# How the recurrent state is turned and split into float16 halves: casts and two transposing transfers, in place of block transposes and a way through DRAM

## Chip, cores and metric

The kernel runs on one core of a Trainium2 chip, alone. The metric is the time of one execution in microseconds (us) of device time; the number given for a kernel is the median of several runs.

## What is computed

Two graph layers work on `x`, 32 batches of 512 nodes with 128 features, over one adjacency matrix `adj` of 512 x 512. Each layer normalises its input, applies a ReLU, and adds its result to its input. Layer 0 is graph attention. Layer 1 is a gated recurrence of five steps, and the change lies in it:

```python
def step(h, _):
    m_in = jnp.einsum('nm,bmd->bnd', in_matrix, h)
    m_out = jnp.einsum('nm,bmd->bnd', out_matrix, h)
    av = jnp.concatenate([m_in, m_out], axis=-1)
    u3 = h @ u3_w.T + u3_b
    z = jax.nn.sigmoid(av @ w3_w.T + w3_b + u3)
    r = jax.nn.sigmoid(av @ w4_w.T + w4_b + u3)
    hv = jnp.tanh(av @ w5_w.T + w5_b + (r * h @ u5_w.T + u5_b))
    h = (1.0 - z) * h + z * hv
    return (h, None)
```

Both matrices are `adj` here, so one product `m` serves for both, with the two halves of each weight added up beforehand.

## The kernel before

**Tiles.** A batch is one tile of 128 partitions x 512 columns. The state `h` of a batch is needed in two layouts. With features on the partitions and nodes along the columns it is `hT` (float32, 128x512); all gates and the update work on that. With nodes on the partitions it is the weight operand of the product with the adjacency, and there it stands as two float16 tiles `hi` and `lo` (128 x 4 x 128): `hi` is `h` rounded to float16, `lo` is what is left, rounded too. Their two products are added in one PSUM bank, so the matmuls run in float16 and the result keeps nearly float32's precision. Ten slots of `hT`, `hi`, `lo` and `x1` (the layer's input) let up to ten batches be under way.

**One step of one batch** (`recurrence`, L1013 to L1222): four matmuls with `hi` and four with `lo` (L1032) make `m`; ACT copies it to `mT` (L1043); two matmuls make the gate `r` (L1051, L1052), ACT takes the tanh (L1057), DVE makes `rh` (L1064); a third matmul makes `z` (L1072), ACT its tanh (L1084); two matmuls make the candidate `v` (L1095, L1096), ACT takes its tanh (L1102), and three DVE instructions update `hT` (L1109, L1115, L1118). Then `hT` has to be turned for the next step.

**Three ways of turning.** For the first batches and for the last two steps of the last four batches, TensorE transposes `hT` into PSUM (L1156). The very last batch has an `ending` of its own (L1224), in two half tiles. All other steps, 118 before a next step and 28 after the last one, go this way: DVE transposes 32x32 blocks (L1170, tile `blocks`), SP stores them to a DRAM tile `way` (L1176), and four loads on SP bring them back with the blocks in place (L1181, tile `rows`, 32 partitions each). Where a next step follows, `halves` (L1002) makes `hi` from `rows` on ACT (L1009) and `lo` on DVE (L1007). After the last step, ACT (L1205) and DVE (L1208) make the result from `rows` and SP stores it (L1221). Layer 0 has a similar way of its own, through the POOL queue (L734, L747), and is not touched.

**The order of the work** is not left to a scheduler. Every piece of work is a `Task` with an engine, a cost from the table `COST`, its needs, its buffers, a key (when it is due) and `lands`, the delay after which others see its result. `plan` (L84) plays the tasks forward: at each turn it takes, on the engine that can begin first, the task with the lowest key among those that can begin nearly as early, and the list of begin times becomes the fixed program order of each engine. A transfer has `lands=LANDING`, 5000 ns. Sixty-eight dummy transposes (`idle`, L435) have the highest key, so that they are put wherever TensorE has nothing else in the plan. A `Buffer` is taken from a pool whose size stands in `BUFFERS`; the plan waits for one to come free. So a change of one piece of work can give another order everywhere behind it.

```python
order = plan(tasks)
for t in order[:-BRANCH]:
    t.issue()
```

`general_path` is a second way for inputs that break the fast path's assumptions; it is not run with these inputs.

Of the kernel before, what the change touches and what calls it, by code (L numbers as in the profile page):

```python
# [10 lines left out]
F32 = mybir.dt.float32  # L11
F16 = mybir.dt.float16
AF = mybir.ActivationFunctionType
ALU = mybir.AluOpType

P = 128
# [11 lines left out]
SLOTS = 10  # L28
# [18 lines left out]
}  # L47
FIRST_IDLE, IDLE = 32, 36
LANDING = 5000
BRANCH = 150  # L50

WAIT = {"DVE": 200, "ACT": 200}
BANKS = {"m": 2, "g": 3, "v": 2, "o": 4, "bank": 8}
BUFFERS = {
    "x": 4, "h0": 2, "h0T": 2, "hw": 3, "pt0": 2, "pt1": 2, "pt2": 2, "pt3": 2, "o_": 2, "hN": 2,
    "es": 2, "lines": 2, "blocks": 2, "rows": 3, "res": 2, "mT": 4, "r": 2, "rh": 3, "z": 3,
    "hv": 2, "d": 2, "way": 4, "turn": 4, "line": 4,
}


# [224 lines left out]
def gat_then_gated_gnn_kernel(  # L285
# [20 lines left out]
    nc = tc.nc  # L306
    B, N, D = x.shape
# [10 lines left out]
    pools = {  # L318
        n: fast.enter_context(tc.tile_pool(name=f"w{n}", bufs=n)) for n in set(BUFFERS.values())
    }  # L320
    dram = fast.enter_context(tc.tile_pool(name="dram", bufs=4, space=bass.MemoryType.DRAM))
    psum = fast.enter_context(tc.tile_pool(name="psum", bufs=8, space=bass.MemoryType.PSUM))
    pin = tc.keep_in_program_order
    tasks = []

    def add(*args, **kwargs):
        tasks.append(Task(*args, **kwargs))
        return tasks[-1]

    def new(buffer, name, shape=(P, N)):  # L330
        tag = buffer.tags[0]
        if "bank" in buffer.tags:
            buffer.tile = psum.tile([P, N], F32, tag="bank", name=name)
        elif tag in ("way", "turn", "line"):
            buffer.tile = dram.tile(list(shape), F32, tag=tag, name=name)
        else:
            buffer.tile = pools[BUFFERS[tag]].tile(list(shape), F32, tag=tag, name=name)
        return buffer.tile


# [30 lines left out]
    hTs = [state.tile([P, N], F32, name=f"hT_{s}") for s in range(SLOTS)]  # L371

    his = [state.tile([P, K, D], F16, name=f"hi_{s}") for s in range(SLOTS)]
    los = [state.tile([P, K, D], F16, name=f"lo_{s}") for s in range(SLOTS)]
# [15 lines left out]
    def load_x(b, key=None, lands=3000):  # L390
        f = Buffer("x")

        def issue():
            pin(nc.sync.dma_start(out=new(f, f"x_{b}", (P, K, D)), in_=x_r[b]))

        needs = () if key else (bias_loaded,)
        load = add("SP", [1], key or 5 * (b - LEAD) * STEP, issue, needs, (f,), lands=lands)
        return f, load
# [35 lines left out]
    def idle():  # L434
        pin(nc.tensor.transpose((f_idle.tile or new(f_idle, "idle"))[:, :P], ident, ident))  # L435
# [14 lines left out]
    def issue():  # L450
        pin(nc.tensor.matmul(
            new(f_as, "as_ps")[:, : 2 * D], lhsT=ones[0:1, :],
            rhs=avecs.rearrange("o i d -> o (i d)"), start=True, stop=True,
        ))
# [263 lines left out]
    def blockwise(dst, src, which, keys, needs, buffers, by_halves):  # L718
# [11 lines left out]
        def store(g):  # L730
            def issue():
                if way.tile is None:
                    new(way, f"turn_{which}", (K * P, P))
                pin(nc.gpsimd.dma_start(  # L734
                    out=way.tile.rearrange("(e r) (g q) -> g r e q", r=Q, g=G)[g],
                    in_=f.tile[ts(g, Q)].rearrange("r (e q) -> r e q", q=Q),
                ))

            return issue

        stores = []
        for g in range(G):
            stores.append(add("POOL", [1], keys(1), store(g), (t,), (f, way),
                              lands=LANDING))

# [5 lines left out]

        return add("POOL", [1], keys(2), load, stores, (*buffers, way), lands=LANDING + 1500)

# [10 lines left out]
    def layer0(b):  # L764
# [7 lines left out]
        def keys(i):  # L772
            return begin + length * (base[0] + i) / parts
# [77 lines left out]
        else:  # L851
# [11 lines left out]
            def store(k):  # L863
                def issue():
                    if way.tile is None:
                        new(way, f"line_{b}", (K, P))
                    pin(nc.gpsimd.dma_start(
                        out=way.tile[k].rearrange("(g q) -> g q", g=G),
                        in_=f_lines.tile[k * rep :: Q],
                    ))  # L870

                return issue

            stores = []
            for k in range(K):
                stores.append(add("POOL", [1], keys(1), store(k), (t,),
                                  (f_lines, way), lands=LANDING))

# [5 lines left out]

            t = add("POOL", [1], keys(2), spread, stores, (way, f_es), lands=LANDING + 1500)
        base[0] = 15
# [126 lines left out]
    def recurrence(b, step, halved, turned):  # L1013
# [5 lines left out]
        def keys(i):  # L1019
            return key + i * STEP / 4  # L1020

        hT = hTs[b % SLOTS]
# [16 lines left out]
        high, low = halved  # L1039
# [29 lines left out]
        last = step == STEPS - 1  # L1069
# [66 lines left out]
        if near:  # L1136
            t_keep = add("DVE", [512], keys(3.5) - STEP, keep, (t_z,), (f_z, f_d))
            t = add("DVE", [512], keys(5), gated_hv, (t, t_z), (f_z, f_hv))
            turned = add("DVE", [512], keys(5), twice, (t, t_keep), (f_hv, f_d))
            to_turn = f_d  # L1140
        else:
            t = add("DVE", [512], keys(5), differ, (t,), (f_hv, f_d))
            t = add("DVE", [512], keys(5), gated, (t, t_z), (f_z, f_d))
            turned = add("DVE", [512], keys(5), update, (t,), (f_d,))
# [3 lines left out]
        if nth < 5 * SHORT or (step >= STEPS - 2 and b >= B - SHORT_END):  # L1148

            f = Buffer("o", "bank")  # L1150

            def turn():
                h_ps = new(f, f"h_{b}_{step}")
                h = to_turn.tile if to_turn else hT
                for k in range(K):
                    pin(nc.tensor.transpose(h_ps[:, ts(k, P)], h[:, ts(k, P)], ident))  # L1156

            needs = (add("PE", [256] * K, keys(6), turn, (turned,),
                         (f, to_turn) if to_turn else (f,)),)
            view = ("p k d -> p k d", {})  # L1160

            def src():
                return f.tile.rearrange("p (k d) -> p k d", k=K)
        else:


            f_b, way, f = Buffer("blocks"), Buffer("way"), Buffer("rows")

            def blocks():
                pin(nc.vector.transpose(  # L1170
                    new(f_b, f"blocks_{b}_{step}").rearrange("p (g k q) -> p g k q", g=G, k=K),
                    hT.rearrange("p (k g q) -> p g k q", g=G, k=K),
                ))

            def store():
                pin(nc.sync.dma_start(out=new(way, f"way_{b}_{step}"), in_=f_b.tile))  # L1176

            def load(g):
                def issue():
                    rows = f.tile or new(f, f"rows_{b}_{step}", (P, G, N // G))  # L1180
                    pin(nc.sync.dma_start(  # L1181
                        out=rows[ts(g, Q)],
                        in_=way.tile.rearrange("(a q) (g e) -> g q a e", a=G, g=G)[g],
                    ))

                return issue

            t = add("DVE", [512], keys(6), blocks, (turned,), (f_b,))
            t = add("SP", [1], keys(6), store, (t,), (f_b, way), lands=LANDING)
            needs = []  # L1190
            for g in range(G):
                needs.append(add("SP", [1], keys(6), load(g), (t,), (way, f),
                                 lands=LANDING))
            view = ("p k (a q) -> p a k q", {"a": G})

            def src():
                return f.tile.rearrange("p a (k q) -> p a k q", k=K)

        if not last:
            return halves(b, src, keys(8), needs, (f,), view[0], **view[1]), turned  # L1200
        f_res = Buffer("res")

        def lower():
            res = new(f_res, f"res_{b}", (P, K, D))
            pin(nc.scalar.mul(res.rearrange(view[0], **view[1]), src(), 1 / LIFT))  # L1205
# [4 lines left out]
        def result_at_once():  # L1210
            pin(nc.vector.scalar_tensor_tensor(
                new(f_res, f"res_{b}", (P, K, D)), src(), (0.5 if near else 1) / LIFT,
                x1s[b % SLOTS], ALU.mult, ALU.add,
            ))
# [4 lines left out]
        else:  # L1219
            finished[b] = add("DVE", [512], keys(8), result_at_once, needs, (f, f_res))  # L1220
        add("SP", [1], keys(8), lambda: pin(nc.sync.dma_start(out=out_r[b], in_=f_res.tile)),  # L1221
            (finished[b],), (f_res,), lands=LANDING)  # L1222

    def ending(b, keys, t_rh, t_z, buffers):  # L1224

# [82 lines left out]
    for b in range(B):  # L1308
        halved, turned = layer0(b)
        for step in range(STEPS):  # L1310
            made = recurrence(b, step, halved, turned)
            if made:
                halved, turned = made
# [4 lines that stand above are left out]
    general = nc.values_load(flag[0:1, 0:1])  # L1318
    for t in order[-BRANCH:]:
        t.issue()  # L1320
# [44 lines left out]
```

## Time and profile before

| what | value |
|---|---|
| median of 3 runs | 1141.48 us (1141.41 to 1142.08) |
| span of the profiled execution, first to last instruction | 1139.7 us |
| TensorE (PE) busy | 1133.1 us, 99% |
| VectorE (DVE) busy | 946.9 us, 83% |
| ScalarE (ACT) busy | 659.3 us, 58% |
| GpSimd (POOL) busy | 350.7 us, 31% |
| moved by DMA | 132.88 MB |
| of that, `way` and `rows` | 146 transfers of 256 KB and 584 of 64 KB |
| mean granted TensorE clock | 0.999 |

The span is what the profile sees; the difference of 1.8 us to the median lies ahead of the first instruction and behind the last. The engines work in parallel, so their busy times do not add up to the span; an engine's time counts only where something else waits for it. A row of the profile names a line of the kernel, the engine, the operation, the tile written and the tiles read, the shape and the count; then come the busy time, the mean duration in ns, and the idle time of the engine ahead of these instructions with what ended it. A float32 matmul of the program appears as two records of the profile, a float16 one as one. SPq is the queue in which SP issues transfers.

### The profile page before, as it was taken

How to read it: one execution, taken by the hardware profiler on the slowest of the kernel's cores; microseconds unless marked ns; L12 is line 12 of the kernel's file. 1: busy time of each engine (PE TensorE's matmuls, PEld its weight loads, DVE VectorE, ACT ScalarE, POOL GpSimd, SP SyncE). 2: the span in 40 equal slices, each digit the busy share in tenths (PEclk: the TensorE clock that was granted, in tenths of full speed). 3: DMA queues.
4: the chain of work that ended last, by engine and by line, in shares of the span. 5: the costliest groups of instructions: out<-in, count | busy, mean ns of one | idle time of the engine just before them, and what ended most of it. 6: DMA issues, size and time to landing. Idle time of an engine off the chain costs nothing.

```text
span 1139.7 us, 15186 instructions
## 1 busy us (share of the span) xinstructions
PE 1133.1 (99%) x4373; PEld 599.0 (53%) x4373; DVE 946.9 (83%) x2124; ACT 659.3 (58%) x1297; POOL 350.7 (31%) x503
## 2 busy tenths in 40 slices
PE   9999999999999999999999999999999999999998
PEld 8665554555455545555554555546555555444444
DVE  7888988889789888987898878989898998765764
ACT  6755566555755665564656645575656655554553
POOL 4345324132424234341443315243455321100000
PEclk9999999999999999999999999999999999999999
DMA  3114435353445444443444435444445433332311
GB/s 107 45 49 118 131 106 145 109 142 114 139 115 151 121 139 130 125 125 111 141 138 138 122 110 146 144 132 129 131 128 154 129 103 103 103 98 76 112 37 66
DMA packets 133915, 132.88 MB, mean 117 GB/s; under 512 B 22082, under 2 KB 97988, under 8 KB 133700
## 3 DMA queue, kind: packets, MB, share of 16 engines
q1 hardware_dynamic: 116066, 94.89, 26.6%
q0 software_dynamic: 17472, 36.79, 13.1%
q8 instruction: 36, 0.59, 0.2%
q14 instruction: 51, 0.42, 0.1%
q10 hardware_dynamic: 290, 0.20, 0.1%
HBM read 70.39 MB, written 61.40 MB: 116 GB/s over the span
## 4 chain that ended last, share of the span: by engine, by line
PE 99%; ACT 0%; DVE 0%; issue 0%; POOL 0%; POOLq 0%; DVEq 0%
PE m L1032 24%; PE g L1072 12%; PE g L1051 12%; PE g L1052 12%; PE v L1096 12%; PE v L1095 12%; PE av L923 10%; PE hp L807 3%; PE idle L435 1%; PE h L1156 0%; PE t_a L702 0%; PE t_b L702 0%; PE v_end L1256 0%; PE es L842 0%; PE end L1274 0%; PE at_ps L489 0%
## 5 line engine op out<-in xcount | busy, mean ns | idle before, releaser
L1057 ACT ACTIVATE rs<-g,zrb 128x512 f32<-128x512 f32 x160 | 109.8, 686 | 142.0 <-PE g L1052 138.7
L1102 ACT ACTIVATE hv<-v,vb 128x512 f32<-128x512 f32 x159 | 109.0, 686 | 124.1 <-PE v L1096 123.8
L1051 PE MATMUL g<-hT,u3T 128*128 128x512 f32 x320 | 163.5, 592 | 0.0
L1052 PE MATMUL g<-mT,w4sT 128*128 128x512 f32 x320 | 163.4, 592 | 0.0
L1072 PE MATMUL g<-mT,w3dT 128*128 128x512 f32 x320 | 163.2, 594 | 0.0
L1032 PE MATMUL m<-adjT,hi 128*128 128x512 f16 x640 | 162.4, 379 | 0.0
L1095 PE MATMUL v<-mT,w5sT 128*128 128x512 f32 x318 | 162.4, 592 | 0.0
L1096 PE MATMUL v<-rh,u5hT 128*128 128x512 f32 x318 | 162.4, 592 | 0.0
L1032 PE MATMUL m<-adjT,lo 128*128 128x512 f16 x640 | 161.5, 379 | 0.0
L1043 ACT COPY mT<-m 128x512 f32<-128x512 f32 x160 | 93.6, 585 | 113.6 <-PE m L1032 112.8
L1064 DVE SCALAR_TENSOR_TENSOR rh<-rs,hT 128x512 f32<-128x512 f32 x160 | 108.5, 682 | 54.3 <-ACT rs L1057 53.8
L1109 DVE SCALAR_TENSOR_TENSOR d<-hv,hT 128x512 f32<-128x512 f32 x158 | 107.5, 681 | 54.4 <-ACT hv L1102 53.9
L1084 ACT ACTIVATE zs<-g,zrb 128x512 f32<-128x512 f32 x160 | 109.7, 685 | 64.0 <-PE g L1072 63.1
L923 PEld LDWEIGHTS av<-hw,pt 128*128 128x128 f32 x1024 | 122.2, 191 | 16.6 <-issue 12.7
L923 PE MATMUL av<-hw,pt 128*128 128x129 f32 x1024 | 123.8, 275 | 0.2 <-ACT adjT L498 0.2
L1118 DVE SCALAR_TENSOR_TENSOR hT<-d,hT 128x512 f32<-128x512 f32 x158 | 109.2, 691 | 11.8 <-PE m L1032 0.5
L1032 PEld LDWEIGHTS <-hi 128*128 128x128 f16 x640 | 62.6, 98 | 102.2 <-issue 49.5
L1115 DVE SCALAR_TENSOR_TENSOR d<-zs,d 128x512 f32<-128x512 f32 x158 | 109.1, 691 | 4.8
L1032 PEld LDWEIGHTS <-lo 128*128 128x128 f16 x640 | 62.7, 98 | 88.1 <-issue 22.7
L645 POOL TENSOR_TENSOR rs_b<-ve_b,mhalf 128x4 f32<-128x4 f32 x32 | 36.2, 1132 | 228.2 <-DVE ve_b L625 195.2
L1170 DVE STREAM_TRANSPOSE blocks<-hT 128x512 f32<-128x512 f32 x146 | 102.8, 706 | 4.1 <-DMA way<-blocks 1.4
L734 POOL DMA_DIRECT2D turn_b<-blocks_b x112 | 73.8, 664 | 91.0 <-DVE blocks_b L724 89.3
(140 smaller groups left out, 1434.0 us busy)
## 6 DMA issues: line engine op xcount, KB each, us to landing
way<-blocks SPq DMA_DIRECT2D x146, 256.0 KB, 2.0
rows<-way SPq DMA_DIRECT2D x584, 64.0 KB, 2.2
x<-in_x_dram SPq DMA_DIRECT2D x32, 256.0 KB, 2.8
out_dram<-res SPq DMA_DIRECT2D x31, 256.0 KB, 2.0
turn_a<-blocks_a POOLq DMA_DIRECT2D x112, 64.0 KB, 2.2
h0T<-turn_a POOLq DMA_DIRECT2D x28, 256.0 KB, 3.6
es<-line POOLq DMA_DIRECT2D x28, 256.0 KB, 4.0
turn_b<-blocks_b POOLq DMA_DIRECT2D x112, 64.0 KB, 2.5
```

What stands on the lines that cost most here:

```text
L923: pin(nc.tensor.matmul(avs()[:, i, :], lhsT=f_pts[c].tile[:, ts(2 * part + i, P)], rhs=hw()[:, c, : D + 1], start=start, stop=(c == K - 1) ...
L1032: pin(nc.tensor.matmul(f_m.tile, lhsT=part[:, k, :], rhs=adjT[:, k, :], start=(first and k == 0), stop=(not first and k == K - 1),))
L1051: pin(nc.tensor.matmul(g, lhsT=u3T, rhs=hT, start=True, stop=False))
L1052: pin(nc.tensor.matmul(g, lhsT=w4sT, rhs=f_mT.tile, start=False, stop=True))
L1057: pin(nc.scalar.activation(new(f_r, f"rs_{b}_{step}"), f_g.tile, AF.Tanh, bias=rb, scale=0.5))
L1072: pin(nc.tensor.matmul(f_g.tile, lhsT=w3dT, rhs=f_mT.tile, start=False, stop=True, skip_group_check=True))
L1084: pin(nc.scalar.activation(new(f_z, f"zs_{b}_{step}"), f_g.tile, AF.Tanh, bias=zb, scale=0.5))
L1095: pin(nc.tensor.matmul(v, lhsT=w5sT, rhs=f_mT.tile, start=True, stop=False))
L1096: pin(nc.tensor.matmul(v, lhsT=u5hT, rhs=f_rh.tile, start=False, stop=True))
L1102: pin(nc.scalar.activation(new(f_hv, f"hv_{b}_{step}"), f_v.tile, AF.Tanh, bias=vb))
L1115: pin(nc.vector.scalar_tensor_tensor(d, f_z.tile, 1.0, d, ALU.add, ALU.mult))
L1118: pin(nc.vector.scalar_tensor_tensor(hT, f_d.tile, 0.5, hT, ALU.mult, ALU.add))
```

## The change

For the 118 turns that a next step follows, a new function `crossed` takes the place of block transpose, DRAM tile and `halves`. ACT first casts `hT`, not yet turned, to float16 (`hiT`), DVE subtracts and rounds the rest to float16 (`loT`), and two transposing transfers on SP write `hi` and `lo` from these, SBUF to SBUF, 128 KB each. The plan holds their landing at 3600 ns. Each of the two new tiles has three buffers. The 28 turns after a last step keep the old way, and so do the turns on TensorE.

```diff
 LANDING = 5000
+CROSSING = 3600
...
-    "hv": 2, "d": 2, "way": 4, "turn": 4, "line": 4,
+    "hv": 2, "d": 2, "way": 4, "turn": 4, "line": 4, "hiT": 3, "loT": 3,
...
-    def new(buffer, name, shape=(P, N)):
+    def new(buffer, name, shape=(P, N), dtype=F32):
...
-            buffer.tile = pools[BUFFERS[tag]].tile(list(shape), F32, tag=tag, name=name)
+            buffer.tile = pools[BUFFERS[tag]].tile(list(shape), dtype, tag=tag, name=name)
...
+        elif not last:
+            return crossed(b, step, keys, turned), turned
         else:
...
+    def crossed(b, step, keys, turned):
+
+        hT = hTs[b % SLOTS]
+        f_hi, f_lo = Buffer("hiT"), Buffer("loT")
+
+        def high():
+            pin(nc.scalar.copy(new(f_hi, f"hiT_{b}_{step}", dtype=F16), hT))
+
+        def low():
+            pin(nc.vector.tensor_tensor(
+                new(f_lo, f"loT_{b}_{step}", dtype=F16), hT, f_hi.tile, ALU.subtract
+            ))
+
+        def cross(dst, f):
+            return lambda: pin(nc.sync.dma_start_transpose(out=dst[b % SLOTS], in_=f.tile))
+
+        t_hi = add("ACT", [480], keys(6), high, (turned,), (f_hi,))
+        t_lo = add("DVE", [512], keys(6), low, (t_hi,), (f_hi, f_lo))
+        return (
+            add("SP", [1], keys(6), cross(his, f_hi), (t_hi,), (f_hi,), lands=CROSSING),
+            add("SP", [1], keys(6), cross(los, f_lo), (t_lo,), (f_lo,), lands=CROSSING),
+        )
```

## Prediction

> **What bounds the kernel now.** I read the page's busy times first, then the windows by stage, then the chain.
>
> ```profile
> PE 1133.1 (99%) x4373; PEld 599.0 (53%) x4373; DVE 946.9 (83%) x2124; ACT 659.3 (58%) x1297; POOL 350.7 (31%) x503
> ...
> 0.00:30.00 30.00, 28.48 (x210) 25.60 (x211) 24.07 (x106) 19.81 (x61) 11.50 (x25) 1.00 0.33 102
> 600.00:800.00 200.00, 200.00 (x754) 103.99 (x753) 173.42 (x391) 118.43 (x232) 68.75 (x98) 1.00 0.45 130
> 1125.00:1140.00 15.00, 9.66 (x41) 5.88 (x39) 6.88 (x12) 4.79 (x8) 0.00 (x0) 0.94 0.21 73
> ...
> PE 99%; ACT 0%; DVE 0%; issue 0%; POOL 0%; POOLq 0%; DVEq 0%
> ```
>
> In a window row the first number after the comma is PE's busy time. PE is never idle from 30 to 1125 us; all it lacks are 1.5 us at the start and 5.3 us at the end, 6.8 us in all. The clock is granted in full (1.00). So PE's own work sets the time, and the change leaves that work alone: the built programs hold the same matmuls, and the same 68 dummies. The turns that it touches lie between 104.9 us (first cast of `rows`) and 1084.7 us (last), away from both idle stretches. So little can be gained; the question is what may make PE wait.
>
> **What goes and comes.** The rows of the parts concerned:
>
> ```profile
> L1170 DVE STREAM_TRANSPOSE blocks<-hT 128x512 f32<-128x512 f32 x146 | 102.8, 706 | 4.1 <-DMA way<-blocks 1.4
> L1007 DVE TENSOR_TENSOR lo<-rows,hi 128x512 f16<-128x512 f32 x118 | 80.4, 681 | 16.3 <-ACT hi L1009 12.1 <-DMA rows<-way 3.1
> L1009 ACT CAST hi<-rows 128x512 f16<-128x512 f32 x118 | 72.2, 612 | 0.0
> ...
> way<-blocks SPq DMA_DIRECT2D x146, 256.0 KB, 2.0
> rows<-way SPq DMA_DIRECT2D x584, 64.0 KB, 2.2
> es<-line POOLq DMA_DIRECT2D x28, 256.0 KB, 4.0
> ```
>
> The last number of a transfer's row is the time to landing. *Removed:* 118 block transposes x 706 ns = 83 us of DVE; 118 stores and 472 loads on SP, at 0.34 us and 0.44 us of issue (timeline of SP's queue) 118 x (0.34 + 4 x 0.44) = 248 us of SP. All of it lies beside PE's unbroken work, worth **0 us**. *Kept:* one ACT cast and one DVE subtraction per turn, now from `hT`; I keep 612 and 681 ns. *Added:* 236 transposing transfers. No row shows one.
>
> **Step 1: is a turned half in time?** PE runs in program order, so a late `hi` stops everything behind it. In the built order of the changed kernel I counted, for each of the 118 turns, the matmuls that PE has to do between the last `v` of a step and the first `hi` matmul of the next. Prices come from the chain's shares: 12.0% of 1139.7 us over 160 is 0.855 us for a float32 512, 24.2% over 1280 is 0.215 us for a float16 512, 10.1% over 512 is 0.225 us for an `av` product. The tightest is batch 30 after step 0: 7 x 0.855 + 4 x 0.215 + 8 x 0.225 = **8.65 us**. Next come 9.4 (batch 31 step 1, 14 step 0, 21 step 0) and 10.4 (batch 31 step 0); the other 113 have 14.7 or more, the median is 30. Before, the smallest was 17.2.
>
> From that window comes off what leads to the transfer. The timeline of an undisturbed tail of a step (`v` issued at 1115.46, 1.02 long; `hv` 1116.53, then 1117.24, 1117.97, 1118.77 for the three DVE updates, 0.69 each) takes 1119.46 - 1116.31 = 3.15 us from PE being free to `hT` ready; with the 0.61 us cast 3.8 us. So issue plus landing may take 8.65 - 3.8 = **4.85 us** before PE waits at all, and 5.6 to 6.6 at the other four. `lo` starts 0.7 us later and is needed four matmuls (0.86 us) later: the same, if the queue is free.
>
> Bounds for issue plus landing from rows: from below the `way` store, 0.34 + 2.0 = 2.3 us, for twice the bytes. From above layer 0's full way through DRAM on POOL: 2.63 us for four issues, 2.5 to land, then 0.79 and 3.5 = 9.4 us. The nearest are single transfers of a 128x512 tile, 2.3 to 4.6 (`es`: 0.58 + 4.0); I take 3 to 4. That is under 4.85, so PE waits for none: **0 us**. The cover is these windows; at 9.4 us it is gone by 4.5 + 3.8 + 3.7 + 3.7 + 2.8 = 18.5 us, each a stall that nothing gives back.
>
> **Step 2: does SP keep up?** 118 turns in 980 us are one in 8.3 us, with two transfers each. Up to 8.3 / 2 = 4.15 us of a transfer that excludes the next one, the queue drains. Issue costs 0.34 us (a 128-partition copy) to 1.75 us (a tile in four pieces), both far under it: **0 us**. Behind a waiting transfer on SP stand x loads, result stores, and the old way of the 28 last turns; no matmul waits closely for those. POOL's queue is not passed by anything. The cast gains a wait too: each new tile has three buffers, so ACT waits, with all that is queued behind, for a transfer three turns back, 3 x 8.3 = 25 us earlier. That is **0 us** as long as a transfer takes less than that.
>
> The Trainium skill weighs in on both sides here. Advanced Engine Details and Errata, section X-Bar Transpose (TRN2), holds such transfers as fast as ordinary ones, 350 to 400 GB/s; 128 KB would be an estimated 0.4 us on top of a fixed part, and step 2 would stand. VectorE: DVE Perf Modes, section The three transpose paths, speaks against the change: 1309 ns by DMA for one 128x128 block against 311 on VectorE. If that were a rate and not a delay, four blocks would be an estimated 5.2 us per transfer, over the limit of step 2. No row here decides between them.
>
> **Step 3: the end.** The plan comes out in another order, and at the very end this shows. Before:
>
> ```profile
> 1129.42 1.02 PE L1096 MATMUL v<-rh,u5hT 128*128 128x512 f32 x2
> 1130.54 0.69 ACT L1102 ACTIVATE hv<-v,vb 128x512 f32<-128x512 f32 x1 [1.09 <-PE v L1096]
> 1131.26 0.69 DVE L1129 SCALAR_TENSOR_TENSOR hv<-zs,hv 128x512 f32<-128x512 f32 x1 [1.09 <-ACT hv L1102]
> 1131.99 0.69 DVE L1132 SCALAR_TENSOR_TENSOR kept<-hv,kept 128x512 f32<-128x512 f32 x1
> 1132.01 1.05 PE L1244 MATMUL end<-minus,kept 128*128 128x128 f32 x8
> 1132.90 0.60 PE L1156 MATMUL h<-ident,kept 128*128 128x128 f32 x4
> 1133.65 1.16 PE L1274 MATMUL end<-plus,gated 128*128 128x128 f32 x8 [0.15 <-DVE gated L1267]
> 1134.85 0.76 DVE L1282 TENSOR_TENSOR res<-end,x 128x256 f32<-128x256 f32 x2 [0.32 <-PE end L1274]
> 1135.63 1.07 SPq L1290 DMA_DIRECT2D out_dram<-res  x1
> ```
>
> Batch 30's candidate `v` comes ahead of batch 31's short ending, so batch 30's long tail (tanh, two DVE steps, turn, result) is covered, and the last store goes at 1135.63. In the changed order 31's `v_end` and `end<-minus` come first, then 30's `v`, then `end<-plus`, four dummies, and 30's turn last. PE's total is the same, so `v` leaves PE at 1134.64 (1134.81 less 0.17: a float32 record is 592 ns long in a slot of 0.855 / 2 = 0.427 us) - 0.15 (the idle) - 0.89 (`end<-plus`, by the distance 1132.01 to 1132.90) - 0.44 - 0.44 (four dummies, four transposes, 0.11 each by 1119.76 to 1120.20 in the timeline) = 1132.72. `end<-plus` is seen at 1133.78, and in the changed DVE order both halves of 31's result stand ahead of 30's `hv` step: until 1134.58. Then 0.69, 0.72 (the start distance above), to 1135.99; the turn begins 0.10 later and ends 1136.69; the result ends 1137.41; the store goes at 1137.43. That is **1.8 us** later than 1135.63. Its 256 KB instead of 128 I cost at nothing: these land in 2.0 (median) against 2.8.
>
> **Sum:** 1139.7 + 0 + 0 + 0 + 1.8 = 1141.5 us of span. The median before lies 1.8 us over the profiled span (1141.48 against 1139.7), so the time is **1143.3 us**, 0.16% more. About 0.2%, 2.3 us, is what a measurement of this kernel can tell from no change.
>
> **Rivals.**
>
> *A, the forecast:* transfers in time, the end 1.8 us longer; alone 1142.6 to 1144.0 (the tail's hand-offs are good to 0.7 us). 48%: 40 within 0.2%, 8 slower.
>
> *B, slower: a landing longer than the windows.* For it: the five windows shrank to 8.65 to 10.4 us because the new order trusts in a fast landing, and SP's queue is in order, so `lo` stands behind `hi`. Against it: every single-tile row is under 4.85. It decides from 4.85 us of issue plus landing at batch 30 step 0, and costs 18.5 us at 9.4: 1144 to 1161.8 us. 28%.
>
> *C, slower: the transfers become the bound.* From 4.15 us apiece SP's queue no longer drains and PE waits for it in all stages. With the `es` row's 4.6 us one after another: 104.9 + 236 x 4.6 + 55 (from 1084.7 to the end) = 1245.5 us of span, 1247 us. For it: nothing in the trace shows that two of them overlap. Against it: ordinary transfers do overlap (four `rows` issues in 1.75 us, landing in 2.2 each). 12%.
>
> *D, the change does less than it says, in the good sense:* the lighter DVE lets the end run without the 1.8 us, or PE's small gaps close. 1138.5 to 1142 us; nothing below that, since PE's work is untouched. 12%: 8 within 0.2%, 4 faster by over 0.2%.
>
> Together: faster 4, within 0.2% 48, slower 48. The likeliest single case is A. The range 1141.5 to 1161.8 leaves out C and most of D.
>
> **What would show it.** PE busy 1133 us again, DVE down by 83 us; the transposing rows landing in 2 to 4 us with issues under 1.8 us; no PE idle between 30 and 1125 us; at the end, batch 30's turn as PE's last work after an idle of about 2 us. It is wrong if PE's weight loads of `hi` or `lo` wait for a transfer (B: in a few places, above all near 950 to 1020 us; C: everywhere), or if PE's busy time moves.

## The result, and the profile after

The changed kernel takes **1143.38 us** (median of 20 runs), the kernel before 1141.55 us in 20 runs beside it: ratio **1.0017**, 95% interval 1.0011 to 1.0023. That is 1.8 us more, at the edge of what a measurement can tell here. The forecast was 1143.3 us. The profiled execution spans 1141.5 us (before: 1139.7) and took 1143.22 us.

The page of the changed kernel, in the parts shown of before:

```profile
PE 1133.2 (99%) x4373; PEld 598.2 (52%) x4373; DVE 875.9 (77%) x2006; ACT 662.0 (58%) x1297; POOL 350.1 (31%) x503
...
PE 96%; DVE 2%; ACT 1%; DMA 0%; issue 0%; POOL 0%; DVEq 0%; POOLq 0%
```

PE's busy time has not moved (1133.1), VectorE's fell by 71 us (the 83 us of block transposes, which I forecast, are a sum of durations; most instructions on VectorE overlap the next one by some 0.08 us in the timeline). In the chain VectorE and ScalarE now hold 2% and 1%: it passes the two waits shown next, and ahead of one of them 25 us of work on VectorE and ScalarE. The rows of the new parts, from the page's groups and the list of transfers (last number: median us from the beginning of the issue to landing):

```profile
L1236 DVE TENSOR_TENSOR loT<-hT,hiT 128x512 f16<-128x512 f32 x118 | 80.8, 686 | 19.0 <-ACT hiT L1233 17.8
...
L1233 ACT CAST hiT<-hT 128x512 f16<-128x512 f32 x118 | 72.7, 616 | 59.7 <-DVE hT L1119 58.9
...
hi<-hiT SPq DMA_TRANSPOSE x118, 2.5
lo<-loT SPq DMA_TRANSPOSE x118, 2.6
```

These are medians, the issue included. The trace gives the landing of 179 of the 236 transposing transfers, and they differ much: 113 took 3 us or less (least 2.4) and 66 took longer, 14 of them longer than 4.85 us, up to 6.5; all 14 were issued before 875 us. While a transfer of POOL's was under way (110 of the 179) the median was 3.4 us, otherwise 2.4. What PE waited for, in the whole execution (us in all, times, longest):

```profile
PE h L1157 <- DVE kept L1133: 1.7, 1, 1.7
...
PE g L1073 <- ACT rs L1058: 0.9, 1, 0.9
...
```

No wait names `hi` or `lo`. Two are new: 1.7 us for `kept` at the end, which the forecast had, and 0.9 us for `rs`, which it had not. The window of its stage (first number after the comma: PE's busy time; in the windows before it PE has no idle):

```profile
800.00:1000.00 200.00, 199.06 (x757) 103.25 (x756) 158.80 (x359) 114.14 (x220) 60.27 (x87) 1.00 0.40 90
```

And the end of the changed kernel, from the timeline, to be held against the nine lines shown of before:

```profile
1131.79 1.02 PE L1096 MATMUL v<-mT,w5sT 128*128 128x512 f32 x2
...
1133.51 1.05 PE L1300 MATMUL end<-plus,gated 128*128 128x128 f32 x8
...
1134.60 0.76 DVE L1308 TENSOR_TENSOR res<-end,x 128x256 f32<-128x256 f32 x2 [1.79 <-PE end L1300]
...
1136.73 0.65 PE L1157 MATMUL h<-ident,kept 128*128 128x128 f32 x4 [1.74 <-DVE kept L1133]
...
1138.14 0.33 SPq L1224 DMA_DIRECT2D out_dram<-res  x1
```

Batch 30's turn is PE's last work after an idle of 1.74 us, and the store that goes last is the one of batch 30.

**A correction that every comparison of profiles here needs.** PE's first matmuls run at half rate, and for how long differs between executions that begin with the same instructions: by an estimate from the distances between the starts of matmuls in the timelines, some 3.5 to 4.5 us or some 8.5 to 9.5. From the timelines of the kernel before, and of the second experiment, whose program begins with the same instructions:

```profile
5.88 1.31 PE L435 MATMUL idle<-ident 128*128 128x128 f32 x10
...
8.65 1.14 PE L807 MATMUL hp<-wrow,h0T 128*128 128x131 f32 x8
```

```profile
6.55 2.40 PE L435 MATMUL idle<-ident 128*128 128x128 f32 x10
...
11.26 1.06 PE L807 MATMUL hp<-wrow,h0T 128*128 128x131 f32 x8
```

The same ten dummies take 1.31 or 2.40 us, so the first `hp` matmul starts at 8.65 or 11.26 us, and PE, hardly ever idle afterwards, does not make it up. So I subtract that start from each span. The times of most kernels fall into two groups some 2 to 3 us apart (before: 15 of 20 near 1141.4 and five near 1143.7); that these are the two lengths of the start fits the nine profiled executions of kernels with ten runs or more, but was not tried by itself.

| kernel | median us (runs) | kernel before beside it | ratio, 95% interval | span | first `hp` | span less start, against before |
|---|---|---|---|---|---|---|
| before | 1141.55 (20) | | | 1139.7 | 8.65 | |
| after | 1143.38 (20) | 1141.55 (20) | 1.0017, 1.0011 to 1.0023 | 1141.5 | 8.50 | +1.95 |
| end mended | 1143.13 (12) | 1143.88 (23) | 1.0004, 0.9994 to 1.0014 | 1140.9 | 8.98 | +0.87 |
| before with the new end | 1145.48 (12) | 1143.88 (23) | 1.0014, 1.0005 to 1.0024 | 1143.8 | 11.26 | +1.49 |
| transfers twice | 1157.18 (4) | 1143.88 (23) | 1.0132, 1.0110 to 1.0154 | 1153.2 | 8.80 | +13.35 |
| transfers four times | 1638.38 (1) | 1143.88 (23) | | 1636.5 | 9.14 | +496 |
| no early PE turns | 1139.77 (11) | 1141.78 (31) | 0.9982, 0.9973 to 0.9991 | 1140.3 | 11.21 | -1.96 |
| before, no early PE turns | 1144.27 (12) | 1141.78 (31) | 1.0013, 1.0004 to 1.0023 | 1142.1 | 10.85 | +0.20 |
| x ahead | 1142.97 (10) | 1141.78 (31) | 1.0012, 1.0003 to 1.0021 | 1141.0 | 8.48 | +1.47 |
| no early PE turns, DIRECT 3 | 1138.37 (7) | 1141.78 (31) | 0.9973, 0.9961 to 0.9984 | 1135.6 | 8.47 | -3.92 |
| slow plan | 1141.02 (10) | 1141.77 (19) | 0.9994, 0.9984 to 1.0005 | 1138.8 | 8.43 | -0.68 |
| x counted slower | 1141.11 (10) | 1141.77 (19) | 0.9992, 0.9982 to 1.0002 | 1139.2 | 8.71 | -0.56 |

Ratios are to runs of the kernel before on the same chip. Medians mix long and short starts in different shares ("end mended" has a lower median than the kernel before beside it, and a ratio of 1.0004), so read the ratios and the last column.

### The profile page after: what moved, and what is told of

Read it like the earlier page. It is cut to its first block, busy times and chain, and to the rows that moved or that the text cites. A ratio compares the mean times of both kernels' runs of the same rounds, so it can differ in the third digit from the quotient of the medians.

```text
span 1141.5 us, 14359 instructions
## 1 busy us (share of the span) xinstructions
PE 1133.2 (99%) x4373; PEld 598.2 (52%) x4373; DVE 875.9 (77%) x2006; ACT 662.0 (58%) x1297; POOL 350.1 (31%) x503
## 2 busy tenths in 40 slices
DMA packets 177334, 101.90 MB, mean 89 GB/s; under 512 B 141026, under 2 KB 156516, under 8 KB 177124
## 4 chain that ended last, share of the span: by engine, by line
PE 96%; DVE 2%; ACT 1%; DMA 0%; issue 0%; POOL 0%; DVEq 0%; POOLq 0%
PE m L1033 23%; PE g L1073 12%; PE v L1097 12%; PE v L1096 12%; PE g L1053 12%; PE g L1052 12%; PE av L924 10%; PE hp L808 2%; PE idle L436 1%; PE h L1157 1%; DMA x<-in_x_dram 0%; ACT h L683 0%; DVE d L1116 0%; DVE hT L1119 0%; DVE pt L893 0%
## 5 line engine op out<-in xcount | busy, mean ns | idle before, releaser
L1233 ACT CAST hiT<-hT 128x512 f16<-128x512 f32 x118 | 72.7, 616 | 59.7 <-DVE hT L1119 58.9
L1053 PEld LDWEIGHTS g<-mT,w4sT 128*128 128x128 f32 x320 | 60.8, 190 | 76.5 <-issue 70.3
```

Source lines behind the costliest of these rows:

```text
L1053: pin(nc.tensor.matmul(g, lhsT=w4sT, rhs=f_mT.tile, start=False, stop=True))
```

## The experiments

Two theories. **O, order:** the transfers cost PE nothing; the loss comes from the order that the plan makes when it is told of a faster turn (the end of the program, and one stall). **T, transfers:** the transposing transfers themselves cost the time, by their 2.5 us each or by what they do to others.

### 1. The end mended (after, batch 30's candidate ahead of batch 31's ending)

```diff
-            u = add("PE", [1024] * 2, keys(3), candidate, (t_rh, *halves_made[-1:]), (f_v, f_mT, f_rh))
+            u = add("PE", [1024] * 2, keys(3), candidate, (t_rh, candidates[b - 1], *halves_made[-1:]), (f_v, f_mT, f_rh))
```

> The changed kernel, with one more need: both halves of batch 31's ending wait in the plan for batch 30's candidate, so that the candidate comes first again, as before the change. Theory O (the order that the plan made costs the time, the transfers themselves nothing): the idle of 1.74 us ahead of batch 30's turn goes, the last store is issued 1.57 us earlier; if the last store's issue grows back from 0.33 to 1.07 us, the span falls by 0.9 only. So 1141.8 to 1142.5 us, span 1139.9 to 1140.6, with the stall of 0.94 us near 831 us still there if it belongs to this order. Theory T (the transposing transfers cost time where they run): no change at the end matters, 1143.4 us.

The wait for `kept` is gone, the 0.9 us for `rs` stays. From the waits, and the last store from the timeline:

```profile
PE g L1073 <- ACT rs L1058: 0.9, 1, 0.9
...
1137.06 1.05 SPq L1316 DMA_DIRECT2D out_dram<-res  x1
```

At the changed kernel's start the span would be 1140.4 us, inside what O gave. From the first `hp` to the issue of the last store: before 1126.98, after 1129.64 (+2.66), here 1128.08 (+1.10). So the end's order costs 1.6 us up to the last issue. Of the span it costs less, 1.95 - 0.87 = 1.1 us, because the changed kernel's last store is the sooner done (below). The 0.94 us stall accounts for what is left.

### 2. The other way round: before, with the new kernel's end

```diff
         kept = add("PE", [512] * K, keys(-1), turn_kept, (t_keep, halves_made[-1]), (f, f_d))
+        candidates[b - 1].needs.append(kept)
+        candidates[b - 1].missing += 1
+        kept.heirs.append(candidates[b - 1])
```

> The kernel before, no transposing transfer in it, with the reverse: batch 30's candidate waits in the plan for the first part of batch 31's ending, as the changed kernel has it by chance. All else stands in the order of before. Theory O: the whole loss of the end appears without the change: the last store is issued 2.2 us later than 1135.63 (by the steps of the prediction without the four dummies, which hide 0.44 us of it), less 0.7 if the last store's issue shortens as in the changed kernel: 1143.0 to 1143.8 us. Theory T: 1141.5 us, as before.

Its end, from the timeline:

```profile
1138.74 0.66 PE L1156 MATMUL h<-ident,kept 128*128 128x128 f32 x4 [2.17 <-DVE kept L1132]
...
1140.16 0.33 SPq L1221 DMA_DIRECT2D out_dram<-res  x1
```

The raw span, 4.1 us longer, looks too large; 2.6 of it are the slower start. The rest is +1.5, and the ratio says +1.6 us (the last store is issued 1.92 us later, counted from the first `hp`; O gave 2.2): without a single transposing transfer, the order of the end alone costs about what O said.

### 3 and 4. Each transposing transfer issued twice, and four times

```diff
-            return lambda: pin(nc.sync.dma_start_transpose(out=dst[b % SLOTS], in_=f.tile))
+            def issue():
+                for _ in range(1):
+                    spare = pools[4].tile([P, K, D], F16, tag="spare", name=f"spare_{b}_{step}")
+                    pin(nc.sync.dma_start_transpose(out=spare, in_=f.tile))
+                pin(nc.sync.dma_start_transpose(out=dst[b % SLOTS], in_=f.tile))
+
+            return issue
```

(`range(3)` for four times; the extra copies go to a tile that nobody reads.)

> The changed kernel in its own order, but each transposing transfer is issued twice, first to a spare tile that nobody reads, then to its place. At 1.20 us of issue each, SP needs 4.8 us per turn of the 8.3 it has; a half lands 1.2 us later, lo 3.6 us. Theory O (SP's issue is the cost, transfers overlap, windows of 4.85 us and more): lo is late by 0.4 us at the tightest window, and where turns bunch up with x loads and result stores behind them a few microseconds come on top: 1144 to 1152 us. Theory T (two such transfers exclude each other, 2.5 us each from issue to landing): four per turn are 10 us of 8.3, and the time is near 105 + 118 x 10 + 55 = 1340 us.

> The changed kernel in its own order, each transposing transfer issued four times, three of them to spare tiles. SP needs 8 x 1.20 = 9.6 us per turn, more than the 8.3 that it has. Theory O: SP's issue is now the bound: 105 + 118 x 9.6 + 55 = 1293 us, and 60 to 80 us for the other transfers that SP issues in that stretch, 1293 to 1400 us. Theory T (exclusive of each other, 2.5 us each): 105 + 118 x 20 + 55 = 2520 us. If neither holds and issues overlap, under 1200 us.

SP's timeline with transfers twice, and of PE's waits the largest group and those that name a transfer:

```profile
975.25 1.27 SPq L1245 DMA_TRANSPOSE hi<-hiT  x1
976.61 1.22 SPq L1244 DMA_TRANSPOSE spare<-loT  x1
```

```profile
PE v L1097 <- DVE rh L1065: 4.3, 2, 3.0
...
PE m L1033 <- DMA lo<-loT: 1.5, 1, 1.5
...
PE m L1033 <- DMA hi<-hiT: 0.5, 1, 0.5
```

One leaves every 1.3 us and lands 2.6 to 3.2 us (medians of the four) after its own issue began: they overlap, and what each takes for itself is 1.3 us of SP's queue. T's 1340 us is refuted; O's upper 1152 is passed, with 1155.04 us for the profiled execution and 1157.18 for the median. The two waits for `hi` and `lo`, at 977 and 979 us, stand before batch 30's second step: the very window that the prediction found tightest. They are 2.0 us of the 11.4 that this kernel's span, less its start, is over the changed kernel's. Three other waits that the changed kernel has not, between 788 and 841 us, make 5.9. Ahead of the longest (3.0) the chain passes a load of `x` that left SP at 833.60, behind eight transposing issues in a row and a store. Most of the rest shows as more busy time of PE (1136.4 us for 1133.2), not as a wait.

Four times is 10.5 us of issues a turn, over the 8.3 us that a turn has; the time goes to 1638 us. T's 2520 is refuted, but O's 1293 to 1400 is too low: 118 x 10.5 + 94 (before the first) + 66 (after the last, as in the changed kernel) = 1399 us holds only for an SP that never waits itself and issues nothing else, and its queue shows 499 us of waits in the whole run, 461 of them for what engines make. In addition PE, busy for 76%, was granted a clock of 0.87. So the issue time alone did not price this queue once it was the bound. It is one run, and what made the engines' results late was not taken apart.

### 5. Early turns taken from PE (end mended, SHORT 0)

```diff
-SHORT = 3
+SHORT = 0
```

(with the edit of experiment 1)

> The changed kernel with the candidate of batch 30 kept ahead of batch 31's short ending (as in the first experiment) and with the early turns of batches 0 to 2, which TensorE made (4 transposes each), handed to the transposing transfers: 6 turns, 24 transposes, fewer on TensorE, 12 transfers more on SP. A turn of 4 transposes takes 0.44 us of TensorE in the trace. If the transfers cost nothing and only the plan's order does, TensorE has 6 x 0.44 = 2.6 us less to do and all of it shows: the span is 2.6 us under the first experiment's 1140.9 us, which began its full-rate matmuls 0.5 us later than the changed kernel's profile did, so 1137.8 to 1138.3 us with a start like the changed kernel's, and a time of 0.9975 to 0.999 of the kernel before. If the transfers themselves cost time, these 12 in the thinnest part of the plan, where few batches are under way, cost most: TensorE waits for hi or lo there, some 2.5 us for each pair, 5 us or more in all, and the time is 1.002 of the kernel before or over.

1139.77 us, 0.9982 (0.9973 to 0.9991): a little faster than before. Less its start the span is 2.83 us under experiment 1 (24 transposes x 0.11 = 2.6), with no wait of PE for `hi` or `lo`. Twelve more transposing transfers in the thinnest part of the plan cost PE nothing that shows; O holds.

### 6. The control: the same in the kernel before

Edit: `SHORT = 0` in the kernel before.

> The control to the run with no TensorE turns early: the kernel before with the same 6 turns handed to its own way, block transposes and two passes through DRAM. TensorE has the same 2.6 us less to do, but the way through DRAM is longer (a transfer to DRAM landed 2.0 us after its issue, those back 2.2 us after theirs, four issues more on SP), and few batches are under way to cover it. If the short way of the transposing transfers is what makes the early turns pay, this kernel gains less than 2.6 us or loses: 0 to 5 us above the kernel before, ratio 1.000 to 1.004, with waits of TensorE in the first 100 us. If both ways are covered alike, it gains the 2.6 us: ratio 0.998.

Ratio 1.0013: no gain. PE lost 1.2 us to waits that the kernel before does not have:

```profile
PE g L1072 <- ACT rs L1057: 0.8, 2, 0.5
PE m L1032 <- DVE lo L1007: 0.4, 1, 0.4
```

The profiled execution shows only +0.2 us; the runs' +1.5 holds more long starts (10 of its 12 runs lie in the upper group, 11 of the 31 beside it), and group against group it is 0.3. Either way the 2.6 us do not come, and only 1.2 of them stand in the waits; the rest is in none that the profile names. So the faster turn has a value here: PE can hand over work to it with a gain that the way through DRAM does not give. Whether another order would let the way through DRAM gain too was not tried.

### 7. The load of x put ahead

```diff
+        if (b, step) == (20, 3):
+            after_x29.extend(pair)
...
+        if b == 29:
+            for u in after_x29:
+                u.needs.append(loaded)
+                u.missing += 1
+                loaded.heirs.append(u)
```

> The first experiment's kernel with one more edit: the load of x of batch 29 is put ahead of the two transposing transfers of batch 20 that SP issued just before it. No other instruction changes its place on any engine. In the changed kernel this load was issued at 801.1 us, landed 4.8 us later, VectorE waited 2.2 us for it, and TensorE stood 0.94 us at 831 us. If the stall comes from the load being late behind the two issues, the load goes out some 2.5 us earlier, VectorE's wait and the 0.94 us are gone, and the span is 0.9 us less than the first experiment's at the same start: 1140.0 us where that began its full-rate matmuls, 1139.5 us where the changed kernel's profile did. If the stall has another source (the load's landing is no cause, or the landing is slow wherever it stands and ends as late), TensorE still waits 0.5 to 0.9 us for rs at 831 us.

First the place in the changed kernel, from its timeline:

```profile
799.79 1.21 SPq L1241 DMA_TRANSPOSE lo<-loT  x1
...
801.10 0.53 SPq L395 DMA_DIRECT2D x<-in_x_dram  x1
...
805.96 0.87 DVE L617 BATCH_NORM_STATS2 st_a<-x 128x6 f32<-128x128 f32 x4 [2.16 <-DMA x<-in_x_dram]
```

Then the same place with x ahead, from its timeline and from the waits of SP's queue:

```profile
800.47 0.33 SPq L395 DMA_DIRECT2D x<-in_x_dram  x1
...
800.91 1.20 SPq L1247 DMA_TRANSPOSE hi<-hiT  x1
...
804.44 0.87 DVE L618 BATCH_NORM_STATS2 st_a<-x 128x6 f32<-128x128 f32 x4 [0.72 <-DMA x<-in_x_dram]
```

```profile
SPq L395 <- DVE x L984: 8.1, 1, 8.1
```

My expectation fell. The load could not go 2.5 us earlier: it waits for its buffer, which VectorE frees at 800.4, so the two issues had held it up by only 0.6 us. VectorE's wait shrank to 0.72 and the 0.94 us stall went, but the two transfers now left 2.4 us later, and two other waits came (0.8 us for `pt`, 0.4 us for `rh`): less the starts, the span is 0.6 us longer than experiment 1's. Going first on SP does not win the 0.94 us; it trades one stall for two.

### 8. One layer more taken from PE (experiment 5, DIRECT 3)

Edit: experiment 5 and `DIRECT = 3` for 4.

> The run with no TensorE turns early, with one more edit: the first layer of batch 3 is turned by block transposes too and not by TensorE (8 transposes fewer, 2 turns of 0.44 us). If TensorE's work alone sets the time, another 0.9 us goes: a span of 1137.0 to 1137.5 us with a start like the changed kernel's, ratio to the kernel before 0.997 to 0.998. If the transfers cost time themselves, it is no better than the run with no TensorE turns early, 1.002 or over.

1138.37 us, ratio **0.9973**, 0.9961 to 0.9984: it beats both kernels. The span came out lower than expected (1135.6), because the 0.9 us stall is gone in this order, too: from 30 to 800 us PE is never idle, and from 800 to 1120 it lacks 0.2 us, with 248 transposing transfers.

### 9. The same transfers under a plan that thinks them slow

```diff
-CROSSING = 3600
+CROSSING = 11500
```

> The changed kernel, with one number altered: the plan counts 11.5 us from the issue of a transposing transfer to its landing and not 3.6 us, about what it counted for the way through DRAM (two transfers of 5.0 us and their issues). The instructions are the changed kernel's; only their order is that of a plan which takes the turn to be as slow as before. If the plan's order alone made the changed kernel later, the end of the program goes back to that of the kernel before, with no wait of TensorE for kept: a span of 1139.2 to 1140.6 us with full-rate matmuls beginning where the profile of the kernel before had them (8.65 us at the first hp matmul), ratio 0.9995 to 1.0010. If the transfers themselves cost time, the order brings nothing back: 1141.5 us or over, ratio 1.0015 or more.

The end stands in before's order again, and PE waits for nothing in between:

```profile
1132.22 0.60 PE L1157 MATMUL h<-ident,kept 128*128 128x128 f32 x4
...
1134.95 0.81 SPq L1316 DMA_DIRECT2D out_dram<-res  x1
```

```profile
PE idle L436 <- POOL ident masks.py:199: 1.4, 1, 1.4
PE av L924 <- ACT adjT L499: 0.2, 1, 0.2
```

Every instruction of the change is there, 236 transposing transfers among them; one planning number differs, and the whole loss is gone (0.9994, 0.9984 to 1.0005). At the kernel before's start the span is 1139.0 us, a little under what O gave. A plan that thinks a transfer slow also gives each one more cover, so this run alone would hide a late landing too. But in the changed kernel PE never waited for `hi` or `lo`, and experiment 2 made the end's loss without any such transfer. Together they decide for O.

### 10. A slower landing of x in the plan (end mended)

```diff
-    def load_x(b, key=None, lands=3000):
+    def load_x(b, key=None, lands=5200):
```

> The first experiment's kernel, with one number altered: the plan counts 5.2 us, not 3.0 us, from the issue of a load of x to its landing (the load whose lateness was followed by the 0.94 us stall took 4.8 us). If that stall is the plan's misjudged landing, the plan places VectorE's work on x later and the stall is gone: the span is 0.9 us under the first experiment's at the same start (1140.6 us there with a start like the kernel before's), so 1139.4 to 1140.0 us. If it is a price of the transfers in that stretch, 0.5 to 1.2 us of waits between 790 and 900 us stay, as they did when the load was put ahead (there 1.2 us, in two waits).

The stall is gone (PE waits for nothing between 30 us and the end), the span 1139.2 us with the first `hp` at 8.71: 0.3 us under what O gave. The plan had trusted in 3.0 us. But the whole order moves with this number, and in this execution no load of `x` after the first 3 us took over 3.6 us (of those whose landing the trace gives). So it shows that another order has no such stall, not that the plan's wrong number made it.

## Why the prediction was right

The number was right (1143.3 against 1143.38) and so was its main reason: PE's work stays, the transfers come in time, and the end's new order costs. But that the number fits so closely is luck, because the sum holds two terms that were not foreseen and nearly cancel. Less the starts, the span grew by 1.95 us: 0.94 (the stall) + 1.72 (the end, up to the last issue) - 0.71 (the last store's close). So the end gave about 1.0 us of the 1.8 forecast for it, and the stall most of the rest.

- **Removed work worth 0: right.** 71 us less of VectorE moved nothing; PE's busy time is 1133 us as before. SP was not even relieved: 236 x 1.20 = 283 us of transposing issues stand for the 248 us removed. (PE lacks 6.6 us before, not 6.8: the last window that I added up reaches 0.3 us past the span.)
- **Step 1, in time: right, in part by luck.** I took 3 to 4 us for issue and landing together, against 4.85 allowed at batch 30 step 0; the median is 2.5, and PE waits for `hi` nowhere. My bounds counted the issue twice: the rows' landing times begin with the issue (a `way` store issued at 499.74 has its loads leave at 501.80, and its row says 2.0). And I compared one landing time with the tightest window, while 14 of the 179 took longer than that window allows. In the window itself `hi`, issued at 963.52 us, took 2.4 us and lay ready 2.2 us before PE came to it; PE waited for none of the long ones. I did not look at POOL's transfers, beside which the landings are longer. When the issues doubled, this was the only window in which PE waited for a half.
- **Step 2, SP keeps up: right in its result, its limit too lenient.** The limit applies to what excludes the next transfer. That is 1.3 us of issue, not the 2.5 to landing; 2 x 1.3 fits into 8.3 us. But already 4 x 1.3 = 5.2 us a turn cost 11 us, of which 8.0 stand in five waits between 788 and 981 us: the queue is in order and not evenly filled, so what stands behind a run of issues comes late. Rival C's premise, transfers one after another, is refuted. The 1309 ns that the Trainium skill gives for one 128x128 block (VectorE: DVE Perf Modes, section The three transpose paths) cannot be read as a rate here: four blocks land in 2.5 us, and the next four follow after 1.3. That such transfers are as fast as ordinary ones (the Trainium skill, Advanced Engine Details and Errata, section X-Bar Transpose (TRN2)) fits the landing, 2.5 us against medians of 2.0 to 2.8 for SP's plain transfers, but not the issue, 1.20 us against 0.33.
- **Step 3, the end: right in mechanism, and in size up to the last issue.** 1.80 us forecast, 1.72 measured (2.66 to the last issue, less the stall's 0.94); experiment 1 takes away 1.56 of it, experiment 2 makes 1.92.
- **Failed in step 3: "Its 256 KB instead of 128 I cost at nothing".** From the last issue to the end of the span before has 4.07 us, after 3.36. Over the profiles of all kernels but the one with four transfers, those which end in two 128 KB stores on two queues, 0.3 us apart, take 3.8 to 4.15 us; those which end in one 256 KB store alone 3.4 to 3.7. The bigger store was the cheaper close; why was not tried.
- **Missing: the 0.94 us stall.** The prediction looked for waits at `hi` and `lo` alone, and said that PE would have no idle between 30 and 1125 us. A new order can be tight anywhere: here VectorE, which works in order, stood 2.16 us for a load that the plan counted as landed after 3.0 us and that took 4.84, and 25 us later PE stood for `rs`. Two other orders of the same instructions (experiments 9 and 10) have no such stall, nor has experiment 8, where a load of `x` took 5.2 us and PE's longest wait between 30 us and the end was 0.2. What slowed this one landing stays open. Beside it `hT` (5.1 us to landing) and `es` (5.0) of POOL and a transposing `lo` (5.4) were under way, all slower than their medians (3.4, 4.1 and 2.6). In the kernel before, no load of `x` after the first 3 us took over 3.6 us; here two took 4.8 and 5.1, and the second cost nothing. So the transposing transfers may have a part in the slow landing, and that it became a stall is this order's.

## What to carry to other kernels

Where one engine is busy for 99% of the span, as PE is here, work taken from the others was worth nothing by itself; what a faster way is worth shows when the full engine hands it work (experiments 5 and 8), and here only the faster way gained by that (experiment 6). A planner that is told of a faster step makes another order, so the change has to be judged apart from the order: keep the operations and restore the planning number, as in experiment 9, and look at the end of the program first. Before differences of 2 us are read from two profiles, hold their first microseconds side by side.

## What the runs showed of the hardware

- A transposing transfer of 128x512 float16 within SBUF takes 1.20 us of SP's issue, against 0.33 for a plain store of a tile; the next can follow after 1.3 us, and the two overlap. It lands 2.4 us after the beginning of its issue when POOL moves nothing, 3.4 us when it does (medians). By estimate 128 KB in 1.3 us is 100 GB/s, as fast as this one queue issued them.
- The number of packets grew by a third (133915 to 177334) while the bytes fell from 132.88 to 101.90 MB; 141026 packets are under 512 bytes. No wait of PE in the changed kernel names one of the new transfers.
- PE's slow start lasts to about 5 us or to about 10.5 us, with 1.00 shown as granted clock. The Trainium skill (TensorE: Matmul & The Clock Gate, section Part 1: The HAM clock gate) tells of a slow start of about 3.4 us that varies from run to run; the variation agrees, but the longer start here is some 9 us of half-rate matmuls.
